# Patch layer of a four-layer network: one quarter of a direction's B products moved to ScalarE and TensorE, with the side work planned anew

## The chip, the cores and the metric

The kernel runs on one core of one Trainium2 chip. The metric is the device time of one execution in microseconds. Five engines work side by side, each through its own queue in order: TensorE (PE in the profile; PEld is its weight load), VectorE (DVE), ScalarE (ACT), GpSimd (POOL) and SyncE (SP), which here only issues DMAs.

## The reference: what is computed

The input is eight images of 96 channels and 64 x 64 pixels. Four layers follow one another, each added to its input. The change touches only the third, the patch layer. For each image it convolves, samples the image at shifted places, and cuts the result into 4 x 4 patches. Each patch is scanned in four directions with its own weights:

```python
def step(hst, inputs):
    ut, dt, bt, ct = inputs
    dA = jnp.exp(dt[..., None] * A)
    hst = hst * dA + (dt * ut)[..., None] * bt[:, :, None, :]
    y = jnp.einsum('bkdn,bkn->bkd', hst, ct)
    return (hst, y)
```

There are 192 inner channels d and 16 states n. So each step needs, for each channel and state, a decay `exp(dt*A)`, a **B product** `(dt*u)*b`, the recurrence, a **C product** `h*c`, and a sum over the states. The four directions are then added, normalised, gated and projected.

## The kernel before, in words

**Chunks and groups.** The patch layer (`layer2`, line 1190) works on 64 chunks: 8 images of 8 chunks, each of 512 pixels (32 patches of 16 steps). A chunk has 48 groups: four directions n = 0 to 3 (12 groups each; n = 0 and 1 form one pair, n = 2 and 3 the other). A group holds 32 channels by 4 states on the 128 partitions and two further sets of states side by side on the free axis, so a tile is 128 x 2 x 512. Two groups (part 0 and part 1) cover the 16 states of 32 channels. A chunk's 48 groups stand in slots B to B+47, with B = 48 times the chunk's number; below, **slot s** means slot B+s, counted modulo 48, as neighbouring chunks overlap. Direction 1 holds slots 6 to 17, direction 3 slots 30 to 41; directions 0 and 2 hold the rest.

**One slot.** `WideSlots.slot` (line 451) issues one slot's work, and each engine runs it in that order:

- SP loads `dd` (the step sizes d and the products d*u, spread over partitions) for the group six slots ahead, one load for two groups.
- ACT computes the two decays of the next group into the PSUM tile `ps_d` (line 466, two instructions of 128 x 512). `ps_d` has three buffers, so they wait for the C product of the group two slots back, which reads the same buffer.
- DVE runs the scan of this group over 1024 elements (line 1584), writing over `ps_d`, and then the C product of the previous group (line 490) into `dbu`.
- PE sums the states of the group two slots back into `ps_y` (line 373, two 512-column matmuls, four records in the trace).
- POOL makes the B product of the group two slots ahead into `dbu` (line 485, 128 x 1024; eight buffers).

`LATE2` names groups whose scan writes over `dbu` instead, whose C product is made by POOL in place, one slot after the scan, and whose sum on PE comes a slot later. It is empty before the change.

**Side work.** All else is planned by hand with `sl.at(slot, engine, function)`. Within a slot the order is: decays, "first" (ACT), scan, sum, "pe", "act", B product, C product, "pool", "dve", "sp". All side matmuls share one PSUM buffer `ps_a`, so each waits until ACT has copied out the one before it. The items that matter here:

- `front`: the offset convolution (line 1280, 18 matmuls), its copies (line 1294), Gelu (line 1312), the two offset rows (lines 1321 and 1332), Tanh (line 1341) with the scaling after it (line 1348), and bilinear sampling on POOL (lines 1359 to 1383). Gelu, Tanh and Silu (line 1469) each come with two activation table loads.
- `inner` and `both` (lines 1403 to 1432): the products u, and the rows b and c, which go to DRAM and come back spread as `brep` and `crep`.
- `pair` (line 1474): the step sizes of two directions by softplus: Abs and Relu (1495, 1496), Exp, add one, Ln, less one (1502 to 1513) on ACT, and four kinds of POOL products on three blocks (lines 1522 to 1538).
- `gates` and `end`: gate, normalisation, output, residual.

Of the kernel before, what the change touches and what calls it, by code (L numbers as in the profile page):

```python
# [13 lines left out]
ALU = mybir.AluOpType  # L14
# [232 lines left out]
AHEAD2, SPREAD2 = 6, 4  # L247
LATE2 = ()

# [192 lines left out]
class WideSlots(Slots):  # L442
# [8 lines left out]
    def slot(self, t):  # L451
        nc, G = self.S.nc, self.groups.get
        g = G(t + self.ahead)
        if g and g.part:
            g.dd = G(t + self.ahead - 1).dd
        elif g:
            g.dd = new(self.pool, [128, 2, NW], "dd", bufs=self.spread)
            nc.sync.dma_start(
                g.dd.rearrange("p x l -> p (x l)"),
                g.steps().unsqueeze(1).to_broadcast([self.gc, 128 // self.gc, 2 * NW]),  # L460
            )
        g = G(t + 1)
        if g:
            g.da = new(self.psd, [128, 2, NW], "ps_d")
            for i in range(2):
                nc.scalar.activation(  # L466
                    g.da[:, i, :], g.dd[:, 0, :], AF.Exp, scale=g.a[:, i : i + 1]
                )
        self.side(t, "first")
        g = G(t)  # L470
        if g:
            g.h = g.dbu if g.late else g.da
            g.scan(*(v.rearrange("p i l -> p (i l)") for v in (g.h, g.da, g.dbu)))
        g = G(t - 2)
        if g and not g.late:
            self.total(g)
        self.side(t, "pe")
        g = G(t - 3)
        if g and g.late:
            self.total(g)  # L480
        self.side(t, "act")
        g = G(t + 2)
        if g:
            g.dbu = new(self.pool, [128, 2, NW], "dbu", bufs=8)
            nc.gpsimd.tensor_tensor(  # L485
                g.dbu, g.dd[:, 1:2, :].to_broadcast([128, 2, NW]), g.b(), ALU.mult
            )
        g = G(t - 1)
        if g:
            (nc.gpsimd if g.late else nc.vector).tensor_tensor(g.dbu, g.h, g.c(), ALU.mult)  # L490
        for engine in ("pool", "dve", "sp", "end"):
            self.side(t, engine)
# [697 lines left out]
def layer2(S, src, dst, st_in, st_out, images, cp, W, ready, finish):  # L1190
# [3 lines left out]
    with ExitStack() as ctx:  # L1194
# [31 lines left out]
        pads, samples = [], []  # L1226
        for k in range(4):
            t = new(cp, [CH, 10, IW + 2], f"pad{k}")
# [15 lines left out]
        def front(ch, b, pad, xs, c, B):  # L1244
# [4 lines left out]
            def load():  # L1249
                ch["x"] = new(fp, [CH, 10 * IW], "xl")  # L1250
                r = 8 * c - 1
# [49 lines left out]
            for m, slots, last in (  # L1301
                (0, ((-81, 1), (-80, 2), (-79, 1), (-78, 1), (-77, 1), (-76, 1), (-75, 2)), -74),
                (1, ((-67, 1), (-66, 2), (-65, 1), (-64, 1), (-63, 1), (-62, 1), (-61, 2)), -60),
            ):
# [9 lines left out]

            sl.at(B - 60, "act", gelu)

            def offset(a):
# [15 lines left out]

                sl.at(B - 59 + a, "pe", pe)
                sl.at(B - 58 + a, "first", act)

# [12 lines left out]

            sl.at(B - 57, "act", tanh)  # L1350
            sl.at(B - 56, "act", place)

# [45 lines left out]
            def inner(j):  # L1398
# [16 lines left out]

                sl.at(B - 23 + j, "pe", pe)
                sl.at(B - 22 + j, "first", act)

# [11 lines left out]
            def both_out():  # L1430
                ch["bc"] = new(fp, [128, NW], "bc")
                nc.scalar.copy(ch["bc"], ch["pa"])
# [4 lines left out]

            sl.at(B - 20, "pe", both)
            sl.at(B - 19, "first", both_out)
            sl.at(B - 19, "sp", both_store)  # L1440

        def gates(ch, pad, T):
            x = pad[:, 1:9, 1 : IW + 1]

            def gate(m):
# [15 lines left out]

                sl.at(T + m, "pe", pe)
                sl.at(T + 1 + m, "first", act)

# [6 lines left out]

            sl.at(T + 2, "act", silu)

        def pair(ch, xs, n, T):
# [4 lines left out]
            def first(j):  # L1479
# [11 lines left out]
                def act():  # L1491
                    if j == 0:
                        st["e"] = new(fp, [128, BLK, NW], "sp_e")
                        st["m"] = new(fp, [128, BLK, NW], "sp_m")
                    nc.scalar.activation(st["e"][:, j, :], st["p"], AF.Abs)
                    nc.scalar.activation(st["m"][:, j, :], st["p"], AF.Relu)

                sl.at(T - 26 + j, "pe", pe)
                sl.at(T - 25 + j, "first", act)

# [14 lines left out]
            for m, run in enumerate((exp, one, ln, less)):  # L1515
                sl.at(T - 22 + m, "act", run)

            def block(j):
                e, m, w, s = (lambda k=k: st[k][:, j, :] for k in "emws")

                def add():
                    nc.gpsimd.tensor_tensor(m(), m(), s(), ALU.add)  # L1522

# [3 lines left out]
                def delta():  # L1527
                    if j == 0:
                        pr["d"] = new(fp, [128, BLK, 2, NW], "delta", bufs=2)
                    nc.gpsimd.tensor_tensor(pr["d"][:, j, 0, :], m(), w(), ALU.subtract)  # L1530

# [16 lines left out]
                for i, run in enumerate((add, lost, delta, delta_u)):  # L1548
                    t = BLK * i + j
                    t = T - 18 + t + (t > 4)  # L1550
                    sl.at(t, "pool", run)
                sl.at(t + 1, "act", edges)

            for j in range(BLK):
                first(j)
                block(j)
            return pr

        def direction(ch, pr, xs, k, n, T):
# [43 lines left out]
            def steps_of(h, g):  # L1603
                row = (n % 2) * DI + h * HD + g * GC2
                j, r = row // 128, row % 128
                return lambda: pr["d"][r : r + GC2, j].rearrange("p x l -> p (x l)")

            for h in range(2):
                for i in range(6):
# [5 lines left out]
                        c=lambda p=part: dr["c"][:, 2 * p : 2 * p + 2, :],  # L1615
                        y=y_of(h, e), scan=scan, late=24 * (n // 2) + 12 * h + e in LATE2,
                    )

        def end(ch, im, b, c, B):
# [64 lines left out]
            def residual():  # L1684
                ch["xo"] = new(fp, [CH, 8, IW], "xo")
                nc.sync.dma_start(
# [38 lines left out]
            for h in range(2):  # L1725
                columns(h)
                centred(h)
                sl.at(B + 76 + h, "pool", lambda h=h: gated(h))
                sl.at(B + 87 + h, "pe", lambda h=h: out(h))
            for t, engine, run in (  # L1730
                (54, "pe", variance), (55, "first", root), (56, "dve", scaled),
                (84, "sp", residual), (89, "pe", plus), (90, "first", sum_out),
                (90, "dve", stats), (91, "sp", store),
            ):
                sl.at(B + t, engine, run)
            if c == NC - 1:
                GroupStats(S, sl, B + 90, st_out[:, b, :], lambda: im["bns"], fp, psa, "ps_a")

# [4 lines left out]
        def piece(n, b, q, m, T0, T):  # L1743
            p, at = {}, slice(q * 1024, q * 1024 + 1024)

            def load():
                p["y"] = new(wp, [128, 1024], "dbu", bufs=8)
                if m < SPREAD2:
# [28 lines left out]
        for n, b in enumerate(images[ready:]):  # L1777
            GroupStats(
                S, sl, 48 * n - 6, st_in[:, b, :], lambda n=n: late_bns[n], fp, psa, "ps_a", nm[b]
            )  # L1780

        for n, b in enumerate(images):
            im = {"bns": new(fp, [CH, NC, 6], f"bns{n % 2}")}
            for c in range(NC):
                i, ch = NC * n + c, {}
                B, pad, xs = PER * i, pads[i % 4], samples[i % 2]
                front(ch, b, pad, xs, c, B)
# [5 lines left out]

                gates(ch, pad, B + (42 if b == images[-1] and c == NC - 1 else 61))
                end(ch, im, b, c, B)
# [443 lines left out]
```

## Time and profile before

| what | value |
|---|---|
| median of 20 runs | 18146.22 us (18098.46 to 18187.52) |
| the profiled execution | 18165.51 us |
| its span, first to last instruction | 18163.7 us |
| first and last scan of the patch layer (line 1584), from the span's start | 3866.8 and 14301.3 us |
| DVE busy over the span | 16214.0 us (89%) |
| POOL busy | 14801.8 us (81%) |
| PE busy | 13670.5 us (75%) |
| ACT busy | 10057.1 us (55%) |

The profiled execution stands 19 us above the median, inside the spread of the runs. The shares over the span are averages over four different layers; the patch layer is the stretch between the two scans in the table, 10434 us. A line of the groups gives: code line, engine, operation, output and inputs, shapes, count, then busy us, mean ns of one, and after the bar the engine's idle time before such instructions. A line of the timeline gives start, duration, engine and instruction, and in brackets the idle time before it. An instruction's recorded time overlaps a little with the next one's on the same engine, so the distance between starts is what one costs in a full queue.

### The profile page before, as it was taken

To read this page: it belongs to the slowest core of one execution; us is meant where nothing else is said; L and a number is where in the kernel's file an instruction comes from. 1 tells how busy PE (TensorE), PEld (TensorE's weight loads), DVE (VectorE), ACT (ScalarE), POOL (GpSimd) and SP (SyncE) were. 2 spreads that over 40 slices of the span, in tenths; PEclk is the share of its full clock that TensorE was granted. 3 is DMA by queue.
4 is the path that set the end of the run, shared out by engine and by line. 5 is a ranking of instruction groups with operands and counts; after the bars stand their busy time and mean duration, and the time that the engine had idled before them with its cause. 6 is when DMAs were issued, how large, how long until landed. Compare 5 with 4: busy or idle time off the path is not lost. (4 is left out here: it accounts for less than half of the span.)

```text
span 18163.7 us, 125849 instructions
## 1 busy us (share of the span) xinstructions
PE 13670.5 (75%) x32964; PEld 4889.5 (27%) x32964; DVE 16214.0 (89%) x11111; ACT 10057.1 (55%) x16056; POOL 14801.8 (81%) x8876
## 2 busy tenths in 40 slices
PE   8999998968888888888888888888888634433332
PEld 2223233722222222222222222222222211111111
DVE  7999998679999999999999999999999766667667
ACT  6777775556666666666666666666666311111100
POOL 7999996059999999999999999999999555565555
PEclk8999998989999999999999999999999866666666
DMA  7888886366566565666656565666656444444444
GB/s 126 149 150 149 150 150 116 64 155 138 131 136 136 132 138 131 137 132 137 135 133 135 132 139 130 137 134 134 137 131 138 111 137 144 140 142 136 136 128 121
DMA packets 802718, 2437.25 MB, mean 134 GB/s; under 512 B 259122, under 2 KB 260863, under 8 KB 734829
## 3 DMA queue, kind: packets, MB, share of 16 engines
q1 hardware_dynamic: 654541, 1976.06, 52.2%
q0 software_dynamic: 147456, 453.13, 8.3%
q8 instruction: 262, 4.29, 0.1%
q14 instruction: 459, 3.76, 0.1%
HBM read 1116.39 MB, written 104.46 MB: 67 GB/s over the span
## 5 line engine op out<-in xcount | busy, mean ns | idle before, releaser
L373 PE MATMUL ps_y<-dbu,k_red 128*96 128x512 f32 x15360 | 7588.9, 619 | 1479.1 <-DVE dbu L490 1430.5
L485 POOL TENSOR_TENSOR dbu<-dd,brep 128x1024 f32<-128x1024 f32 x3072 | 7216.8, 2361 | 223.4 <-PE ps_y L373 106.9
L1584 DVE TENSOR_TENSOR_SCAN ps_d<-ps_d,dbu 128x1024 f32<-128x1024 f32 x3072 | 7015.4, 2284 | 127.0 <-issue 106.9
L466 ACT ACTIVATE ps_d<-dd,l_alog 128x512 f32<-128x512 f32 x6144 | 4241.6, 691 | 3352.9 <-DVE dbu L490 3236.4
L373 PEld LDWEIGHTS ps_y<-dbu,k_red 128*96 128x96 f32 x15360 | 2343.4, 166 | 6386.5 <-DVE dbu L490 3384.6
L490 DVE TENSOR_TENSOR dbu<-ps_d,crep 128x1024 f32<-128x1024 f32 x3072 | 3702.2, 1205 | 0.0
L2073 POOL DMA_INDIRECT v<-t,idx x2304 | 2190.4, 951 | 1594.2 <-DVE s L2100 778.3
L355 POOL TENSOR_TENSOR dbu<-dd,brep 128x1024 f32<-128x1024 f32 x768 | 1793.3, 2353 | 134.5 <-DMA dd<-delta 114.0
L2100 DVE TENSOR_REDUCE s<-v 128x864 f32<-128x3456 f32 x256 | 1555.0, 6074 | 320.3 <-remote 217.5
L2091 DVE TENSOR_TENSOR v<-v,ps_w 128x3456 f32<-128x3456 f32 x256 | 958.3, 3743 | 831.5 <-ACT ps_w L2083 755.3
L735 DVE TENSOR_TENSOR_SCAN ps_d<-ps_d,carry,dbu 128x512 f32<-128x512 f32 x1184 | 1452.8, 1272 | 87.7 <-POOL dbu L355 69.1
L2119 ACT COPY smp<-ps_t 128x768 f32<-128x768 f32 (+1 forms) x512 | 244.4, 529 | 1769.9 <-remote 1031.6
L1280 PE MATMUL ps_a<-pad,woff 96*96 96x512 f32 x2304 | 1145.8, 598 | 26.8 <-ACT pad L1257 24.3
L337 ACT ACTIVATE ps_d<-dd,l_alog 128x512 f32<-128x512 f32 x1536 | 999.2, 681 | 151.7 <-DMA dd<-delta 100.3
L2111 PE MATMUL ps_t<-k_ident,s 128*128 128x128 f32 (+1 forms) x1792 | 321.8, 332 | 930.6 <-issue 565.2
L365 DVE TENSOR_TENSOR dbu<-ps_d,crep 128x512 f32<-128x512 f32 x1344 | 850.5, 674 | 0.0
L1522 POOL TENSOR_TENSOR sp_m<-sp_m,sp_s 128x512 f32<-128x512 f32 x384 | 487.8, 1270 | 370.9 <-ACT sp_s L1510 370.9
L1925 PE MATMUL ps_u<-k_ident,oc 27*128 27x27 f32 x256 | 33.0, 252 | 868.9 <-ACT oc L1920 844.2
L1908 PE MATMUL ps_a<-xpad,l_om 96*27 96x512 f32 x1152 | 590.8, 666 | 3.0 <-issue 2.9
L1280 PEld LDWEIGHTS ps_a<-pad,woff 96*96 96x96 f32 x2304 | 373.5, 164 | 667.8 <-issue 551.5
L2111 PEld LDWEIGHTS ps_t<-k_ident,s 128*128 128x128 f32 (+1 forms) x1792 | 249.6, 169 | 1057.7 <-issue 841.0
L2142 PE MATMUL ps_o<-smp,l_w 128*96 128x512 f32 (+1 forms) x896 | 461.7, 673 | 95.1 <-ACT smp L2119 70.3
(278 smaller groups left out, 15920.3 us busy)
## 6 DMA issues: line engine op xcount, KB each, us to landing
dd<-delta SPq DMA_DIRECT2D x2304, 512.0 KB
brep<-bcd SPq DMA_DIRECT2D x256, 1024.0 KB
crep<-bcd SPq DMA_DIRECT2D x256, 1024.0 KB
v<-t,idx POOLq DMA_INDIRECT x2304
xo<-x SPq DMA_DIRECT2D x128, 192.0 KB
x<-xo SPq DMA_DIRECT2D x128, 192.0 KB
bcd<-bc SPq DMA_DIRECT2D x64, 256.0 KB
xn<-x SPq DMA_DIRECT2D x64, 192.0 KB
```

Of the source, the lines that this page charges most:

```text
L337: nc.scalar.activation(da, g.dd[:, 0, :], AF.Exp, scale=g.a[:, i : i + 1])
L355: nc.gpsimd.tensor_tensor(g.dbu, g.dd[:, 1:2, :].to_broadcast([128, 2, NW]), g.b(), ALU.mult)
L373: self.S.nc.tensor.matmul(y, self.red[:, HD - self.gc * (g.n + 1) : 2 * HD - self.gc * (g.n + 1)], g.dbu[:, i, :], start=first and i == 0, ...
L466: nc.scalar.activation(g.da[:, i, :], g.dd[:, 0, :], AF.Exp, scale=g.a[:, i : i + 1])
L485: nc.gpsimd.tensor_tensor(g.dbu, g.dd[:, 1:2, :].to_broadcast([128, 2, NW]), g.b(), ALU.mult)
L490: (nc.gpsimd if g.late else nc.vector).tensor_tensor(g.dbu, g.h, g.c(), ALU.mult)
L735: nc.vector.tensor_tensor_scan(out, da, dbu, carry[:, n + i : n + i + 1] if c else 0.0, ALU.mult, ALU.add)
L1280: nc.tensor.matmul(ch["pk"][:HD, :], woff[:, k, m * HD : (m + 1) * HD], pad[:, dy : dy + 8, dx : dx + IW], start=k == 0, stop=k == KT - 1,)
L1584: nc.vector.tensor_tensor_scan(out[:, way], da[:, way], dbu[:, way], 0.0, ALU.mult, ALU.add)
L2073: nc.gpsimd.indirect_dma_start(out=st["v"][:, k].rearrange("p q c -> p (q c)"), out_offset=None, in_=flat, in_offset=bass.IndirectOffsetOn ...
L2091: nc.vector.tensor_tensor(v3, v3, ps_w[:, g % 2, j * 4 * KT : (j + 1) * 4 * KT] .unsqueeze(2) .to_broadcast([128, 4 * KT, CH]), ALU.mult,)
L2100: nc.vector.tensor_reduce(st["s"], st["v"].rearrange("p k q c -> p k c q"), mybir.AxisListType.X, ALU.add,)
```

## The change

**A quarter of the B products of directions 1 and 3.** In the six part-1 groups of each of these directions (slots 7, 9, ..., 17 and 31, 33, ..., 41) POOL makes only the first half of the B product (128 x 512). The other half is made with the steps on the partitions:

- `rows` (new, two times a pair): PE transposes d*u of the pair's second direction, four 128 x 128 blocks, and multiplies the sampled pixels with four b columns (two small matmuls) into `ps_a`; ACT copies both out (`turned`, `turnedb`).
- `scaled` (new, 16 times a pair): one ACT copy of 192 elements with a scale per partition, written with a stride of four elements into `prod`.
- `turn` (new, once per such group): four PE transposes of 128 x 128 bring `prod` back into the second half of the `ps_d` tile. They stand in PE's queue ahead of the sum, in the slot before the scan.
- The second decay of such a group goes into the second half of `dbu` (SBUF), and the scan is split into two of 512, the second with the two inputs in exchanged places.

**Five late groups.** `LATE2 = (14, 16, 21, 38, 40)`: five C products of 128 x 1024 a chunk go from DVE to POOL.

**Buffers.** `dbu` has seven buffers instead of eight, there are three padded chunks instead of four, `xl`, `bc` and `xo` share one buffer, and Relu writes straight into `delta` (the tile `sp_m` goes).

**Side work.** Most items get other slots:

| item | slots before | slots after |
|---|---|---|
| convolution, halves 0 and 1 | 15 to 21, 29 to 35 | 22 to 28, 32 to 37 |
| Gelu (ACT) | 36 | 38 |
| offset rows: PE; copy | 37, 38; 38, 39 | 40, 41; 41, 42 |
| Tanh; scaling after it | 39; 40 | 42; 42 |
| u: PE; b and c: PE | 25 to 27; 28 | 16 to 18; 12 |
| gate: PE; Silu | 13, 14; 15 | 2, 5; 9 |
| softplus on ACT, n = 0 / 1 | 26 to 29 / 2 to 5 | 23 to 26 / 47 to 2 |
| softplus on POOL, n = 0 / 1 | 30 to 42 / 6 to 18 | 26 to 37 / 2 to 13 |
| gating on POOL; output on PE | 28, 29; 39 to 41 | 14, 15; 29 to 31 |

```diff
-LATE2 = ()
+LATE2 = (14, 16, 21, 38, 40)
...
+                da = g.dbu if g.turn and i else g.da
+                nc.scalar.activation(da[:, i, :], g.dd[:, 0, :], AF.Exp, scale=g.a[:, i : i + 1])
+            if g.turn:
+                g.turn(g.da[:, 1, :])
...
+            if g.turn:
+                g.scan(g.h[:, 0, :], g.da[:, 0, :], g.dbu[:, 0, :])
+                g.scan(g.h[:, 1, :], g.dbu[:, 1, :], g.da[:, 1, :])
+            else:
+                g.scan(*(v.rearrange("p i l -> p (i l)") for v in (g.h, g.da, g.dbu)))
...
-            g.dbu = new(self.pool, [128, 2, NW], "dbu", bufs=8)
+            g.dbu = new(self.pool, [128, 2, NW], "dbu", bufs=7)
+            n = 1 if g.turn else 2
             nc.gpsimd.tensor_tensor(
-                g.dbu, g.dd[:, 1:2, :].to_broadcast([128, 2, NW]), g.b(), ALU.mult
+                g.dbu[:, :n, :], g.dd[:, 1:2, :].to_broadcast([128, n, NW]), g.b()[:, :n, :],
+                ALU.mult,
             )
...
-            sl.at(B - 60, "act", gelu)
+            sl.at(B - 58, "act", gelu)
...
-            sl.at(B - 57, "act", tanh)
-            sl.at(B - 56, "act", place)
+            sl.at(B - 54, "act", tanh)
+            sl.at(B - 54, "act", place)
...
+            def rows(q):
+                def pe():
+                    pr["pa"] = new(psa, [128, NW], "ps_a")
+                    for k in range(2):
+                        at = slice((2 * q + k) * 128, (2 * q + k + 1) * 128)
+                        for j in range(1, BLK):
+                            c = k * 256 + (j - 1) * 128
+                            nc.tensor.transpose(
+                                pr["pa"][:, c : c + 128], pr["d"][:, j, 1, at], S.ident
+                            )
+                        nc.tensor.matmul(
+                            pr["pa"][:, k * 256 : k * 256 + HS2], xs[:CH, n, at],
+                            bc_w[:, n, 2 * n + 1, 3:NS:4], start=True, stop=True,
+                        )
...
+                sl.at(T - 10 + q, "pe", pe)
+                sl.at(T - 9 + q, "first", act)
...
+            def scaled(m):
...
+                    nc.scalar.activation(
+                        pr["prod"][:, k, :, q], pr["du"][:, k, :], AF.Copy,
+                        scale=pr["bt"][:, k, q : q + 1],
+                    )
...
+            for t, count in (
+                (-7, 2), (-5, 3), (-4, 1), (-3, 1), (-2, 1), (-1, 1), (0, 1), (2, 1), (3, 1),
+                (4, 2), (5, 2),
+            ):
+                for _ in range(count):
+                    sl.at(T + t, "act", scaled(m))
+                    m += 1
...
+            def turn_of(h, g):
+                at = h * HD + g * GC2
+
+                def run(out):
+                    for k in range(4):
+                        nc.tensor.transpose(
+                            out[:, k * 128 : (k + 1) * 128],
+                            pr["prod"][:, k, at : at + GC2, :].rearrange("p c s -> p (c s)"),
+                            S.ident,
+                        )
```

Here T is the pair's first slot: B for directions 0 and 1, B+24 for directions 2 and 3.

## Prediction

> **What bounds the kernel now.** I read the busy times of a stretch inside the patch layer first, then the groups, then the timeline of single slots. In the stretch (columns: us, then PE, PEld, DVE, ACT, POOL busy, granted clock, DMA share, GB/s) DVE is busy 2967 of 3000 us, POOL 2828. Three groups carry it:
>
> ```profile
> 6000.00:9000.00 3000.00, 2532.81 (x5491) 842.67 (x5490) 2967.39 (x1806) 2017.09 (x2909) 2827.86 (x1535) 0.99 0.61 134
> ```
>
> ```profile
> L485 POOL TENSOR_TENSOR dbu<-dd,brep 128x1024 f32<-128x1024 f32 x3072 | 7216.8, 2361 | 223.4 <-PE ps_y L373 106.9
> L1584 DVE TENSOR_TENSOR_SCAN ps_d<-ps_d,dbu 128x1024 f32<-128x1024 f32 x3072 | 7015.4, 2284 | 127.0 <-issue 106.9
> L490 DVE TENSOR_TENSOR dbu<-ps_d,crep 128x1024 f32<-128x1024 f32 x3072 | 3702.2, 1205 | 0.0
> ```
>
> First and last scan start 10434.5 us apart: 3.398 us a slot, 163.1 us a chunk of 48. The timeline shows what a slot is made of, around Gelu and Tanh:
>
> ```profile
> 7251.51 2.29 DVE L1584 TENSOR_TENSOR_SCAN ps_d<-ps_d,dbu 128x1024 f32<-128x1024 f32 x1
> 7253.70 1.21 DVE L490 TENSOR_TENSOR dbu<-ps_d,crep 128x1024 f32<-128x1024 f32 x1
> 7254.82 2.29 DVE L1584 TENSOR_TENSOR_SCAN ps_d<-ps_d,dbu 128x1024 f32<-128x1024 f32 x1
> ...
> 7258.92 2.30 DVE L1584 TENSOR_TENSOR_SCAN ps_d<-ps_d,dbu 128x1024 f32<-128x1024 f32 x1 [0.70 <-issue]
> ```
>
> ```profile
> 7251.63 1.42 ACT L466 ACTIVATE ps_d<-dd,l_alog 128x512 f32<-128x512 f32 x2 [1.90 <-DVE dbu L490]
> 7252.98 0.76 ACT L1294 ACTIVATE off<-ps_a,sh,sc 96x512 f32<-96x512 f32 x1
> 7253.76 1.28 ACT L1312 ACT_TABLE_LOAD   x1
> 7255.05 1.06 ACT L1312 ACTIVATE off<-off 96x1024 f32<-96x1024 f32 x1
> 7256.12 1.28 ACT L1313 ACT_TABLE_LOAD   x1
> 7257.42 1.42 ACT L466 ACTIVATE ps_d<-dd,l_alog 128x512 f32<-128x512 f32 x2
> ...
> 7263.73 0.57 ACT L1332 COPY fr<-ps_a 96x512 f32<-96x512 f32 x1
> ...
> 7267.98 1.41 ACT L466 ACTIVATE ps_d<-dd,l_alog 128x512 f32<-128x512 f32 x2
> 7269.33 1.13 ACT L1348 ACTIVATE fr<-fr,half 96x1024 f32<-96x1024 f32 x1
> ```
>
> A scan costs 2.19 us (start to next start), a C product 1.12, a slot 3.31. ACT's decays start when the C product frees `ps_d`, 0.12 us after a scan starts; a scan can follow 1.50 us after its decays start (7257.42 to 7258.92). So ACT may be some 1.8 us late before DVE waits. Gelu, with two table loads, is later than that: DVE waits 0.70 us. The waits name three such stalls a chunk, 64.0 us in 6000, or 1.74 a chunk. The bound is DVE plus what ACT's table loads add to it.
>
> **The change, part by part, per chunk.**
>
> Late groups: five C products leave DVE, 5 x 1.12 = **-5.6 us**. POOL gets five, at 2.35 us each by the first layer's row for the same product (line 360, 2352 ns), 11.8 us in all.
>
> Turned groups: POOL makes twelve half products less. A half costs about 1.27 (line 1522, 128 x 512), a whole one 2.36: -13.1. POOL's busy time is 2827.86/3000 x 163.1 = 153.7 us a chunk, so it falls to about 152.4. That is still under DVE. A late product must wait for its scan, so POOL loses its lead at slots 15, 17, 22, 39 and 41; in slots 15, 17, 22 and 41 it has 4.7 us of work against 2.2 of DVE, but 2.4 against 3.3 in the slot after, and a B product has two slots until its scan. Covered; if it weren't, each such slot could cost about 1 us. The sum of a late group comes one slot later, and its `dbu` is wanted again two slots after that, so seven buffers suffice.
>
> Split scans: 12 times, two of 512 for one of 1024. The first layer's scans of 512 without carry take 1206 ns (into PSUM) and 1204 (into SBUF), so where an operand lies costs nothing there. Less the overlap of 0.09, 2 x 1.12 - 2.19 = 0.04: **+0.5**. The form with a carry takes 1268 ns, which as a bound gives +2.0; no row has the inputs exchanged. I take 0.5, the form without carry being the one used.
>
> Work on ACT: 32 scaled copies of 192 elements. The copy at line 1396 reads with a stride of 16 bytes and takes 1.10 us for 512, the scaling at line 1348 takes 1.13 for 1024 contiguous. Counting from the 32-element copy of line 1546 (0.24 us), that gives 0.53 or 0.38 for 192, less 0.1 of overlap 0.43 or 0.28. I take 0.43, as the stride is the same: 13.8 us, and 2 for the copies of `rows`. ACT was busy 109.7 of 163.1. They are spread one to three a slot; where softplus stands too (slots 47 to 2) a slot holds 1.35 of decays, 1.49 at most of softplus and 0.43: 3.27 of 3.31. Hidden, by 0.04. From 0.6 us a copy it would begin to show, about 0.5 us a chunk.
>
> The Trainium skill ("SBUF — State Buffer", "Door 1: The DMA port swizzle") says that SBUF has lines of 16 bytes and wants two hits a line, which speaks against a write with 16 bytes between elements. Here the row at line 1396 agrees for reads: about 1.8 ns an element against 0.9. Without the rule's penalty the copies would be 9 us by the row of line 1348, with it 13.8 by that of line 1396; either is hidden.
>
> Work on PE: 64 transposes and 16 small records. The trace has transposes only in the last layer:
>
> ```profile
> 17496.69 1.70 PE L2111 MATMUL ps_t<-k_ident,s 128*96 128x128 f32 x14
> 17506.87 1.70 PE L2111 MATMUL ps_t<-k_ident,s 128*96 128x128 f32 x7 [8.49 <-DVE s L2100]
> ```
>
> In a stream one costs 0.12 us, after an 8.5 us pause 0.24. I take 0.12: in the patch layer the granted clock is 0.99 and PE pauses little. The tightest place is slots 14 to 17. From scan 14: turn 0.5, skip term 0.9, sum 1.7, `rows` 1.2, sum 1.7, `rows` 1.2, turn 0.5 plus 0.3 to land: 8.0 us, with 8.9 until scan 17 (3.32 + 2.24 + 3.32). Hidden by 0.9.
>
> Table loads: here the cost lies. Stalls of today go (**-1.74**): Silu, in slot 9, stands behind the normalising product (1.2 us on DVE in slot 8), and 3.7 us of it fit. But Gelu and Tanh now stand beside late groups, in which DVE has less to do.
>
> - Gelu, slot 38. Today scan 36 to the scan after Gelu takes 7258.92 - 7251.51 = 7.41 us. In slot 37 a copy that waits for PE and two edge copies now end 0.5 after the decays could start, one edge copy (0.2) is added, and one decay goes to SBUF (about 0.1 less): 8.0. DVE needs 3.32 + 2.24 until scan 40, as the C product of group 38 is POOL's: 5.6. Stall **2.4**.
> - Tanh, slot 42, now with its scaling in the same slot. From scan 41, PE finishes the first offset row (1.0), a sum (1.7), and the second row (1.7 + 0.3); its copy starts at 4.8. From there to the decays 4.25 (7263.73 to 7267.98), the scaling 1.04, decays to scan 1.50: scan 44 at 11.6. DVE alone: 2.24 + 3.32 + 3.32 = 8.9. Stall **2.7**, or 2.1 if PE were never late (the copy after two decays, the first copy and two scaled ones, at 4.2).
>
> New stalls 5.1. Convolution, u, gates and output keep their instructions and DMAs; their new slots fall where ACT and PE have room. The shared `xl` buffer makes SP wait for a store issued 11 slots before. DMA share (0.61) hardly moves.
>
> **Sum:** -5.6 + 0.5 - 1.74 + 5.1 = -1.75 us a chunk, x 64 = -112; before the first slot, ten scaled copies add 4 at most, which I leave out. From the profiled execution, 18165.5 - 112 = 18053; it stands 19 above the median, so the prediction on the median is 18146 - 112 = **18034**.
>
> **Rivals.**
>
> 1. *Transposes cost PE too much (slower).* Place: slots 14 to 17 and 38 to 41, 16 transposes each. At 0.24 each, 16 x 0.12 = 1.9 more: the first place misses by 1.0, the second adds up to 1.9 to the Tanh chain, 2.9 in all, so +1.2 a chunk: **18220**. It turns at 0.20 a transpose (32 x 0.08 less the margin of 0.9 is 1.75). For it: they come in bursts of four behind waits. Against: the stream of fourteen, and the clock. By the Trainium skill ("TensorE: Matmul & The Clock Gate", "Part 4: PE-mode transpose") a transpose takes about 275 ns in a kernel; an estimate from that figure puts the change at a loss of some 150 us. The row of fourteen in 1.70 us contradicts it for a stream.
> 2. *Table loads stall no more than today.* If ACT gets ahead during the stalled scans more than I see, the two stalls stay at 0.7 each: -5.6 + 0.5 - 1.74 + 1.4 = -5.4, **17800**. Against: the queue in order, which today gives its 0.70.
> 3. *No gain to be measured.* The two halves of a `ps_d` or `dbu` tile wait for each other, so that the transposes follow the first decay (0.8 later, once in each tight place), or the copies cost 0.6 to 0.7: 1 to 1.6 us of the 1.75 given back, **18100 to 18140**. Against: today loads and edge copies of different blocks of `delta` don't stall one another.
>
> **How the numbers follow.** Forecast (-60 to -190 us) 0.52; rival 2 (-190 to -350) 0.13; rival 3 0.18, of which 0.02 is still faster by more than 0.2%; rival 1 0.17. A measurement of this kernel can tell about 0.2%, 36 us, from no change. Faster 0.67, same 0.16, slower 0.17. Range: from 17890, half way to rival 2, to 18220, rival 1's own price.
>
> **What would show it.** Scan to scan in a chunk: slots 15, 17, 22, 39, 41 near 2.2, Silu's stall gone, waits of 2 to 3 us before scans 40 and 44 with ACT's table loads ahead of them. If waits before scans 7 to 17 name PE's transposes, rival 1 is right. If the waits are under 1 us, rival 2. POOL idle must not shrink to nothing.

## The result, and the profile after

The changed kernel takes **18383.84 us** (median of 7 runs, 18350.1 to 18401.84), the kernel before beside it 18141.12 (47 runs): ratio 1.0131, 95% interval 1.0118 to 1.0143. It is 243 us slower; 112 us faster was forecast. The profiled execution took 18412.51 us, 247 more than the one of before. Between the first and the last scan of the patch layer lie 10653.2 us against 10434.4: 219 of the 247 are there. The first scan starts 11 us later, and some 17 are behind the last.

The same stretch as before, columns as there (us, then PE, PEld, DVE, ACT, POOL busy, granted clock, DMA share, GB/s):

```profile
6000.00:9000.00 3000.00, 2661.42 (x6798) 1048.14 (x6798) 2829.05 (x1888) 2231.22 (x3567) 2740.84 (x1588) 0.95 0.60 132
```

DVE is busy 138 us less, though the layer lasts longer, so it waits. The granted clock fell from 0.99 to 0.95. The groups of the page:

```profile
L491 POOL TENSOR_TENSOR dbu<-dd,brep 128x1024 f32<-128x1024 f32 (+1 forms) x3072 | 6408.7, 2096 | 120.6 <-ACT ps_d L467 96.4
L1638 DVE TENSOR_TENSOR_SCAN ps_d<-ps_d,dbu 128x1024 f32<-128x1024 f32 (+1 forms) x2752 | 5460.9, 1986 | 370.1 <-issue 271.3
L1596 ACT ACTIVATE prod<-turned,turnedb 128x192 f32<-128x192 f32 x2048 | 1150.7, 628 | 0.0
L497 POOL TENSOR_TENSOR dbu<-dbu,crep 128x1024 f32<-128x1024 f32 x320 | 755.3, 2360 | 342.1 <-DVE dbu L1638 342.1
L1638 DVE TENSOR_TENSOR_SCAN dbu<-ps_d,dbu 128x1024 f32<-128x1024 f32 x320 | 728.5, 2276 | 148.3 <-ACT ps_d L467 148.3
```

The idle time of DVE ahead of scans was 127 us; now it is 370 ahead of those into `ps_d` and 148 ahead of the late ones, which are counted apart. Where it lies in a chunk is read from the distances between scan starts. Below, "slot n" is the distance from scan n to scan n+1, the median over chunks 10 to 54; a full slot is 3.32.

| slot | before | forecast | after | e3 (below) |
|---|---|---|---|---|
| turned, not late (7, 9, 11, 13, 31, 35, 37) | 3.32 (37: 4.10) | 3.36 | 3.58 | 3.58 |
| behind a late group, no wait: 22; with a turned scan 15, 17, 41 | 3.32 | 2.2 | 2.20; 2.46 | 2.20; 2.46 |
| 16 (before: stall behind Silu) | 3.91 | 3.32 | 3.30 | 3.30 |
| 26 | 3.32 | 3.32 | **4.84** | 3.32 |
| 39 (Gelu) | 3.32 | 4.6 | 4.94 | 4.94 |
| 43 (Tanh) | 3.31 | 6.0 | **8.10** | 5.30 |
| mean chunk | 163.1 | 161.3 | 166.9 | 162.9 |

DVE's timeline around Gelu and Tanh, in chunk 25 (scan 39 is the pair at 8183.75, scan 44 the last line):

```profile
8183.75 1.22 DVE L1638 TENSOR_TENSOR_SCAN ps_d<-ps_d,dbu 128x512 f32<-128x512 f32 x1
8185.08 1.23 DVE L1638 TENSOR_TENSOR_SCAN ps_d<-dbu,ps_d 128x512 f32<-128x512 f32 x1
8188.69 2.29 DVE L1638 TENSOR_TENSOR_SCAN dbu<-ps_d,dbu 128x1024 f32<-128x1024 f32 x1 [2.39 <-ACT ps_d L467]
...
8200.02 1.21 DVE L497 TENSOR_TENSOR dbu<-ps_d,crep 128x1024 f32<-128x1024 f32 x1
8205.90 2.30 DVE L1638 TENSOR_TENSOR_SCAN ps_d<-ps_d,dbu 128x1024 f32<-128x1024 f32 x1 [4.67 <-issue]
```

DVE waits 2.39 us behind Gelu, as forecast, and 4.67 behind Tanh, 2 more than forecast. PE's timeline in the same place shows why:

```profile
8184.96 1.94 PE L373 MATMUL ps_y<-dbu,k_red 128*96 128x512 f32 x4
8189.11 0.50 PE L1569 MATMUL ps_a<-k_ident,delta 128*128 128x128 f32 x2 [2.22 <-ACT turnedb L1583]
...
8191.33 3.62 PE L1328 MATMUL ps_a<-off,l_off 96*96 96x512 f32 x4
8194.75 2.60 PE L373 MATMUL ps_y<-dbu,k_red 128*96 128x512 f32 x4
8197.18 1.88 PE L1328 MATMUL ps_a<-off,l_off 96*96 96x512 f32 x4
```

The same four matmuls of an offset row take 3.62 us the first time and 1.88 the second. Four stretches of that place, with the columns of the stretch above (the clock is third from the end):

```profile
8185.94:8189.36 3.42, 1.20 (x5) 0.35 (x4) 1.03 (x2) 3.38 (x6) 3.42 (x2) 1.00 1.02 183
8189.36:8192.77 3.41, 3.41 (x14) 2.46 (x13) 3.41 (x3) 2.77 (x6) 2.12 (x2) 0.50 0.71 240
8192.77:8196.18 3.41, 3.41 (x5) 1.13 (x4) 3.31 (x3) 1.19 (x3) 2.95 (x2) 0.50 0.63 123
8196.18:8200.00 3.82, 3.82 (x10) 1.47 (x9) 3.82 (x3) 2.39 (x5) 2.52 (x2) 1.00 0.24 60
```

The clock is halved for 6.83 us, two stretches of 3.41. In the 3.41 us ahead of them PE stood still for 2.22, since the second `rows` needs `ps_a`, whose copy by ACT stands behind Gelu. In the first half-rate stretch PE is busy all the time, up to 8191.33 with transposes and small matmuls alone, and the clock stays at half for another. The first offset row takes 1.7 us longer, the sum behind it 0.7, and Tanh waits for the second row, which stands behind both.

The other new stall, in slot 26, has the same root. All engines, slots 21 to 26 of the same chunk:

```profile
8127.42 1.96 PE L1287 MATMUL ps_a<-pad,woff 96*96 96x512 f32 x4
8131.02 3.46 PE L373 MATMUL ps_y<-dbu,k_red 128*96 128x512 f32 x4 [1.65 <-DVE dbu L497]
...
8139.01 0.58 ACT L1693 COPY yy<-ps_y 96x512 f32<-96x512 f32 x1 [3.27 <-PE ps_y L373]
...
8142.36 2.30 DVE L1638 TENSOR_TENSOR_SCAN ps_d<-ps_d,dbu 128x1024 f32<-128x1024 f32 x1 [1.44 <-POOL delta L1530]
```

PE waits 1.65 us for a C product, beside the late group 21; the next sum takes 3.46 us instead of 1.88, at a granted clock of 0.51 from 8131.4 to 8134.8. The copy of the patch columns (`yy`) waits 3.27 us for PE at the head of ACT's queue, the last parts of softplus stand behind it, and POOL and DVE wait for those. The trace's clock records, over 44 chunks, have a half-rate stretch of 3.41 us that begins in slot 24 in 39 of them, and one of 6.59 on average in slot 40 in 43. Before, neither place has one. The chunks themselves show what a stretch costs: slot 26 lasts 4.84 or more in the 39 chunks with one in slot 24, and 3.32 in the five without; slot 43 lasts 8.12 (median) in the 40 chunks with 6.83 us at half rate, 6.43 in the three with 3.41, and 5.23 in the one without. Half-rate stretches elsewhere, such as those that begin in slot 45 in 40 chunks, leave their slots at 3.32.

### The profile page after: what moved, and what is told of

The parts are those of the page before. It is cut to its first block, busy times and chain, and to the rows that moved or that the text cites. A ratio compares the mean times of both kernels' runs of the same rounds, so it can differ in the third digit from the quotient of the medians.

```text
span 18410.7 us, 139011 instructions
## 1 busy us (share of the span) xinstructions
PE 14313.7 (78%) x38084; PEld 5681.3 (31%) x38084; DVE 15971.3 (87%) x11559; ACT 10979.4 (60%) x18616; POOL 14728.8 (80%) x9195
## 4 chain that ended last, share of the span: by engine, by line
PE 28%; DVE 25%; ACT 20%; issue 14%; another core or an unknown queue 10%; DMA 2%; POOL 1%; DVEq 0%; SPq 0%; ACTq 0%; POOLq 0%
DVE ps_d L1638 12%; PE ps_y L373 11%; DVE dbu L497 7%; ACT ps_d L467 5%; PE ps_a L1977 2%; ACT prod L1596 2%; PE ps_a L1328 2%; PE ps_k L644 2%; DMA dd<-delta 2%; DVE ps_d L742 1%; PE ps_d L1667 1%; DVE v L2160 1%; DVE s L2169 1%; ACT sp_s L1517 1%
## 5 line engine op out<-in xcount | busy, mean ns | idle before, releaser
L491 POOL TENSOR_TENSOR dbu<-dd,brep 128x1024 f32<-128x1024 f32 (+1 forms) x3072 | 6408.7, 2096 | 120.6 <-ACT ps_d L467 96.4
L1638 DVE TENSOR_TENSOR_SCAN ps_d<-ps_d,dbu 128x1024 f32<-128x1024 f32 (+1 forms) x2752 | 5460.9, 1986 | 370.1 <-issue 271.3
L467 ACT ACTIVATE ps_d<-dd,l_alog 128x512 f32<-128x512 f32 x5376 | 3714.9, 691 | 1741.0 <-DVE dbu L497 1142.7
L355 POOL TENSOR_TENSOR dbu<-dd,brep 128x1024 f32<-128x1024 f32 x768 | 1794.1, 2355 | 142.8 <-DMA dd<-delta 109.7
L1596 ACT ACTIVATE prod<-turned,turnedb 128x192 f32<-128x192 f32 x2048 | 1150.7, 628 | 0.0
L337 ACT ACTIVATE ps_d<-dd,l_alog 128x512 f32<-128x512 f32 x1536 | 999.4, 681 | 164.7 <-DMA dd<-delta 111.7
L497 POOL TENSOR_TENSOR dbu<-dbu,crep 128x1024 f32<-128x1024 f32 x320 | 755.3, 2360 | 342.1 <-DVE dbu L1638 342.1
L1638 DVE TENSOR_TENSOR_SCAN ps_d<-dbu,ps_d 128x512 f32<-128x512 f32 x768 | 943.8, 1229 | 76.8 <-ACT ps_d L467 1.8
L1667 PE MATMUL ps_d<-k_ident,prod 128*128 128x128 f32 x3072 | 543.1, 303 | 513.9 <-ACT ps_d L467 504.9
L1638 DVE TENSOR_TENSOR_SCAN dbu<-ps_d,dbu 128x1024 f32<-128x1024 f32 x320 | 728.5, 2276 | 148.3 <-ACT ps_d L467 148.3
L1530 POOL TENSOR_TENSOR delta<-delta,sp_s 128x512 f32<-128x512 f32 x384 | 489.5, 1275 | 365.6 <-ACT sp_s L1517 365.6
```

The costliest lines, as they stand in the source:

```text
L355: nc.gpsimd.tensor_tensor(g.dbu, g.dd[:, 1:2, :].to_broadcast([128, 2, NW]), g.b(), ALU.mult)
L467: nc.scalar.activation(da[:, i, :], g.dd[:, 0, :], AF.Exp, scale=g.a[:, i : i + 1])
L491: nc.gpsimd.tensor_tensor(g.dbu[:, :n, :], g.dd[:, 1:2, :].to_broadcast([128, n, NW]), g.b()[:, :n, :], ALU.mult,)
L1596: nc.scalar.activation(pr["prod"][:, k, :, q], pr["du"][:, k, :], AF.Copy, scale=pr["bt"][:, k, q : q + 1],)
L1638: nc.vector.tensor_tensor_scan(out[:, way], da[:, way], dbu[:, way], 0.0, ALU.mult, ALU.add)
```

## The experiments

The experiments ran on several chips. On those of e5 to e8 and of e9 and e10 the kernel before takes 17306 and 17302 us, on the others 18121 to 18152. e3 and e8, the same kernel but for hidden copies, have chunks of 162.87 and 162.90 us on two of them, so chunks are compared directly, and times as ratios to the kernel before on the same chip.

**e1 and e2: what does a split scan cost?** Both are the kernel before with the changed kernel's twelve split scans alone; e2 also exchanges `da` and `dbu` in the second (the edit shown is that of e1).

```diff
+            if g.split:
+                g.scan(g.h[:, 0, :], g.da[:, 0, :], g.dbu[:, 0, :])
+                g.scan(g.h[:, 1, :], g.da[:, 1, :], g.dbu[:, 1, :])
```

> The kernel before, with one edit: in the twelve part-1 groups a chunk of directions 1 and 3 the scan of 1024 is issued as two of 512, each half with the inputs in their usual places. In the changed kernel such a split scan takes 2.46 us to the next instruction, where I had reckoned 2.24. Theory A (the exchanged inputs of the second scan, or its two producers, keep it from overlapping the first): here a split scan costs 2.24, 0.04 more than a whole one, 0.5 us a chunk and some 30 us in all, 18170. Theory B (any second scan of 512 waits for the first to drain): 2.46 here too, 3.1 us a chunk, 200 us in all, 18340.

> As the split run, but the second scan of each such group takes its two inputs in exchanged places: first the B product from SBUF, then the decay from PSUM. It computes a wrong recurrence in these halves (decay and product trade roles); its time is what counts. Both halves still come from the same engines as before the change. If the exchange is guilty: 1.32 us from the first scan to the second, 2.46 for both, 3.1 us a chunk, 18340. If it is not the exchange but the two producers (PE and ACT) that the second scan waits for in the changed kernel: 2.24 and 18170, as in the plain split if theory A holds.

e1: ratio 1.0066 (1.0043 to 1.0089), e2 1.0074 (1.0053 to 1.0094), so 119 and 134 us more. The times lie between the two theories. The exchange costs nothing, the split does: in both a turned slot lasts 3.52, and the second scan starts 1.253 us after the first. The changed kernel first, then e1:

```profile
8075.21 1.21 DVE L1638 TENSOR_TENSOR_SCAN ps_d<-ps_d,dbu 128x512 f32<-128x512 f32 x1
8076.52 1.23 DVE L1638 TENSOR_TENSOR_SCAN ps_d<-dbu,ps_d 128x512 f32<-128x512 f32 x1
8077.66 1.21 DVE L497 TENSOR_TENSOR dbu<-ps_d,crep 128x1024 f32<-128x1024 f32 x1
```

```profile
8105.25 2.48 DVE L1588 TENSOR_TENSOR_SCAN ps_d<-ps_d,dbu 128x512 f32<-128x512 f32 x2
8107.64 1.21 DVE L494 TENSOR_TENSOR dbu<-ps_d,crep 128x1024 f32<-128x1024 f32 x1
```

From the first half to the C product it is 2.45 us in the one and 2.39 in the other, where an unsplit scan takes 2.19. In the trace the second half waits on DVE's own count of finished instructions. In the changed kernel it mostly waits for ACT as well, through a semaphore instruction between the halves: the 705 pairs with one start 1.323 us apart, the 63 without, all in slot 33, 1.245. The chunk of e1 is 164.9, and the stalls of before in slots 16 and 40 shrank by 0.2, which gave some of it back.

**e7: is it the shared tile?** The kernel before, in which every group's `ps_d` is two tiles of 512 and every scan and C product is split.

```diff
-            g.da = new(self.psd, [128, 2, NW], "ps_d")
+            g.da = [new(self.psd, [128, NW], f"ps_d{i}") for i in range(2)]
...
+            for i in range(2):
+                g.scan(g.da[i], g.da[i], g.dbu[:, i, :])
```

> The kernel before with the two halves of every ps_d tile as two tiles of 512 (same banks, three buffers each), so that all scans and all C products are issued as two of 512. In the split run the second scan waited 1.25 us after the first began, with a wait for DVE's own count ahead of it; in the first layer, whose halves are two tiles, 1.13 without such a wait. Theory I (the wait comes from both halves being one tile, so that the second half waits for the first to drain): 1.12 to 1.14 here. Theory J (something else of this layer, such as the reversed order or the shapes): 1.25. The C products also come in two, so the kernel is slower either way: 0.04 for the scans and 0.06 to 0.2 for the products in each of 48 slots, 18450 to 18900.

A single run took 17515.33 us, 1.012 of before, less than was expected. The halves now follow each other as in the first layer:

```profile
8100.73 2.33 DVE L1585 TENSOR_TENSOR_SCAN ps_d<-ps_d,dbu 128x512 f32<-128x512 f32 x2
8102.97 1.26 DVE L491 TENSOR_TENSOR dbu<-ps_d,crep 128x512 f32<-128x512 f32 x2
```

A pair takes 2.24, its halves start 1.13 apart, and the wait on DVE's own count is gone in all but 56 of the 3072 pairs. So 0.12 us comes with the two halves being one `ps_d` tile, and some 0.07 more in the changed kernel with the semaphore instruction. Not every shared tile does this: the late groups of the first layer scan into the two halves of one `dbu` tile in SBUF, and there the second half does not wait for DVE and starts 1.14 us after the first (16 pairs without carry, kernel before). Why the PSUM tile does and the SBUF tile doesn't, no run shows. The kernel of e7 is slower because all 48 groups pay: a slot is 3.43.

**e3: the clock.** The changed kernel with matmuls of zero weights, which add nothing to the sums, in PE's two pauses: two behind a convolution matmul of slot 23, three in slot 39.

```diff
+                        if m == 0 and k == 1:
+                            for _ in range(2):
+                                nc.tensor.matmul(
+                                    ch["pk"][:HD, :], zero, pad[:, 0:8, 0:IW], start=False, stop=False
+                                )
...
+                    for _ in range(3):
+                        nc.tensor.matmul(ch["y", 1][:HD, :], zero, xs[:CH, 0, :], start=False, stop=False)
```

> The changed kernel plus matmuls with zero weights in the two pauses of PE that stand before its half-rate windows: two after the second convolution tap (slot 23), added into the open group in ps_a, and three after the sum in slot 39, added into ps_y. They add zeros and change nothing in the output. Theory C (the pauses halve TensorE's granted clock, and the slow matmuls behind them make the stalls): the granted clock in the patch layer goes from 0.95 to about 0.99, the wait of 1.5 us in slot 26 goes, the one before scan 44 falls from 4.8 to about 2.7 us; -3.6 us a chunk, -230 in all, 18150. Theory D (PE is short of time there, whatever its clock): ten more records cost 4.3 us of PE a chunk in the two places, the stalls stay or grow; 18384 or up to 18600.

18143.13 us, ratio 0.9995 (0.9982 to 1.0007): more work on PE makes the kernel some 240 us faster. The same stretch, and scan 44 of chunk 25:

```profile
6000.00:9000.00 3000.00, 2706.13 (x7154) 1059.70 (x7153) 2901.20 (x1939) 2292.61 (x3656) 2811.51 (x1632) 0.98 0.61 135
```

```profile
8106.72 2.30 DVE L1645 TENSOR_TENSOR_SCAN ps_d<-ps_d,dbu 128x1024 f32<-128x1024 f32 x1 [1.90 <-issue]
```

The half-rate stretches of slots 24 and 40 are gone from all 44 chunks, slot 26 is 3.32 again, without a wait, and Tanh's stall is 1.98. Gelu's stays at 2.5: PE has no part in it.

**e4: do transposes hold the clock up?** The changed kernel with its 64 transposes as ordinary matmuls with the identity.

```diff
-                        nc.tensor.transpose(
+                        nc.tensor.matmul(
...
-                            S.ident,
+                            S.ident, start=True, stop=True,
```

> The changed kernel with its 64 transposes a chunk issued as ordinary matmuls against the identity (same output, two records each instead of one, so 7 us more of PE work a chunk). In the changed kernel the second half-rate stretch (slots 40 and 41) lasts two windows of 3.4 us although PE is full in the first of them, with transposes and small matmuls. Theory E (transposes do not count as activity for the clock): the stretch shrinks to one window and the wait before scan 44 from 4.8 to about 3.5 us; the added PE work stays mostly covered; 18300 to 18380. Theory F (the clock does not distinguish them): the stretch stays at 6.8 us, and the added records cost as rival 1 reckoned, 1 to 3 us a chunk; 18450 to 18580.

18413.42 us, ratio 1.0145 (1.0124 to 1.0165), between the two ranges and no faster, though the clock rose to 0.98: the stretches at slot 40 are gone, and Tanh's slot falls from 8.10 to 5.83. But slot 16 becomes 5.03 and slot 39 5.41, and slot 26 stays at 4.85, as its pause has no transposes in it. What the longer stay on PE costs at slots 14 to 17 is the place of rival 1. PE's pause ahead of slot 40 (here in chunk 25):

```profile
8189.23 0.71 PE L1569 MATMUL ps_a<-k_ident,delta 128*128 128x128 f32 x4 [1.22 <-ACT turnedb L1584]
```

It is 1.22 us instead of 2.22, as the matmuls take longer. So e4 alone doesn't tell whether transposes don't count as work where the clock is decided, or the pause was too short. The changed kernel's own trace, over the same 44 chunks, speaks for the first. Cut into windows of 3.41 us, it has 43 at half rate that begin in slot 40: PE is busy for 0.98 or more of each, with matmuls of 512 columns for 0.45 (median), and after 40 of them the next window is at half rate too. After the 151 windows at half rate that matmuls of 512 columns fill to 0.97 or more, the next is always at full rate. The matmuls of four columns that stand between the transposes aren't told apart from them.

**e5 and e6: the late groups alone,** on the kernel before, three and five of them (two edits, in this order).

```diff
-LATE2 = ()
+LATE2 = (13, 21, 28)
...
-LATE2 = ()
+LATE2 = (14, 16, 21, 38, 40)
```

> The kernel before with one edit: LATE2 = (13, 21, 28), three late groups a chunk, none next to an activation table load; nothing is turned and no side work moved. POOL gets 3 x 2.31 = 6.9 us on its 153.7 a chunk, 160.6 in all. Theory G (the late groups carry the whole gain of the change, and POOL can take three without the turned products): DVE loses 3 x 1.12 = 3.4 us of 163.1, POOL's 160.6 becomes the limit or nearly; 160.1 to 160.8 a chunk, 150 to 190 us less, 17960 to 18000. Theory H (late products make POOL lose its lead and DVE waits for B products, or PE pauses and its clock halves): no gain or a loss, 18150 to 18300.

> The kernel before with the change's five late groups alone, LATE2 = (14, 16, 21, 38, 40). POOL's work would be 153.7 + 5 x 2.31 = 165.3 us a chunk, over today's 163.1. Theory G: POOL is the limit, 165 us a chunk, 18230 to 18290. If POOL's two spare slots are enough cover after all, DVE's 163.1 - 5.6 plus the stalls of Gelu and Tanh beside late groups (5.1 less today's 1.4) decides: 161.2, 18030.

e5: **0.990** (0.9884 to 0.9917), a chunk of 160.4; it beats both kernels. e6: 1.0061 (1.0045 to 1.0078), a chunk of 164.9. Both are where theory G put them. Their stretches, in this order:

```profile
6000.00:9000.00 3000.00, 2581.50 (x5598) 885.10 (x5597) 2956.08 (x1779) 2049.23 (x2961) 2998.81 (x1616) 0.97 0.61 137
```

```profile
6000.00:9000.00 3000.00, 2496.42 (x5427) 855.24 (x5426) 2857.96 (x1696) 1988.53 (x2882) 3000.00 (x1612) 0.98 0.61 134
```

POOL is busy 2998.81 and 3000.00 of 3000 us. Three late products just fill it; with five DVE waits for it, in slots 18 to 20 above all. So the exchange that the change makes (POOL gives half products to ACT to take C products) has a reason, but three of the five late groups could be had without it.

**e8: are the scaled copies hidden?** e3 without them; `prod` holds zeros, so a quarter of the B products of directions 1 and 3 is left out.

```diff
-                        pr["prod"] = new(fp, [128, 4, DI, HS2], "prod")
+            pr["prod"] = still
```

> The kernel of the run with zero-weight matmuls in PE's pauses, without the 32 scaled copies a chunk: prod is zeroed once and the transposes turn zeros, so that a quarter of the B products of directions 1 and 3 is left out. If ScalarE's scaled copies (0.43 us each, 13.6 a chunk) are hidden, as I reckoned: no change, 18130 to 18145. If they cost what they take in the crowded slots: up to 3 us a chunk less, 17950.

0.9995 (0.9986 to 1.0005), a chunk of 162.90, the same slots as e3. Hidden.

**e9 to e12: which late groups earn their 1.12 us?** All are e3 with another `LATE2`.

> The changed kernel with the five zero-weight matmuls of e3 in PE's two pauses, and with the late groups 38 and 40 put elsewhere: late are 14, 16, 19, 21 and 45. Theory J (a late group beside a table load saves nothing: ACT sets the time there, so the wait of DVE grows by what its late product frees): each of the two groups now saves its 1.12 us, the waits before scans 40 and 44 shrink by 1.12 each (of 2.48 and 1.98), so the chunk falls from e3's 162.87 to 160.6 us, ratio to the kernel before 0.986. Theory K (the waits are ACT's own and keep their size wherever the late groups stand): the chunk stays at 162.9, ratio 0.9995. Theory L (POOL lacks room for four late products in eight slots): waits of DVE for POOL in slots 20 to 25 and a chunk between 161.5 and 162.5.

> As e9, but the late groups 38 and 40 are left out instead of moved: late are 14, 16 and 21, so DVE makes two products more a chunk. Theory J: these two saved nothing, so the chunk stays at e3's 162.87 us within 0.3 and the ratio to the kernel before at 0.9995 within 0.002; the waits before scans 40 and 44 are 1.12 shorter each. Theory K: DVE has 2 x 1.12 more, the chunk is 165.1, ratio 1.013.

> The changed kernel with the five zero-weight matmuls of e3, and one late group moved: 38, which stands beside Gelu, gives way to 45 (late: 14, 16, 21, 40, 45). By e9 and e10 a late group 38 saves nothing (Gelu's wait shrank by 1.12 when it went), a late group 40 saves its 1.12 (Tanh's wait did not shrink), group 45 saved its 1.12, and the wait before scan 27 in e9 came from POOL, a product behind after groups 19 and 21. Theory M (so read, each group counts by its own place): the chunk falls from e3's 162.87 to 161.75, the slot before scan 40 from 4.94 to 3.8 plus the 1.12 that slot 39 gets back in DVE work, and slot 26 stays at 3.32; ratio to the kernel before 0.9925. Theory N (any further shift of POOL's work brings another wait of 1 to 2 us): 162.9 to 164, ratio 0.9995 to 1.005.

> As e11, with the other of the two groups moved: 40 gives way to 45 (late: 14, 16, 21, 38, 45). In e9, e10 and e11 the six slots from scan 38 to scan 44 last 23.98 us each time, whatever DVE has to do in them, in e3 22.63: the sum of a late group 38 goes to PE a slot later, so the offset matmuls come 1.35 sooner. Theory P (this stretch is a chain of PE and ACT, and group 40 saves nothing in it): it stays at 22.63 without the late group 40, and group 45 saves 1.12, of which 0.75 may be given back in slot 47 as in e11: 161.75 to 162.5 us a chunk, ratio 0.993 to 0.998. Theory Q (group 40 saves its 1.12 and Tanh's wait keeps its size, as I read e10 at first): the stretch lasts 23.75, the chunk 162.9 to 163.6, ratio 0.9995 to 1.003.

| run | late | ratio | chunk | slots 14 to 26 | slots 38 to 43 | slots 44 to 47 |
|---|---|---|---|---|---|---|
| e3 | 14, 16, 21, 38, 40 | 0.9995 (0.9982 to 1.0007) | 162.87 | 40.2 | 22.63 | 13.29 |
| e10 | 14, 16, 21 | 1.0047 (1.0031 to 1.0064) | 164.25 | 40.2 | 23.98 | 13.29 |
| e11 | 14, 16, 21, 40, 45 | 1.0044 (1.0030 to 1.0058) | 163.84 | 40.2 | 23.98 | 12.91 |
| e12 | 14, 16, 21, 38, 45 | 1.0032 (1.0016 to 1.0047) | 163.83 | 40.2 | 23.44 | 13.41 |
| e9 | 14, 16, 19, 21, 45 | 1.0046 (1.0029 to 1.0063) | 164.12 | 41.1 | 23.98 | 12.14 |

Of all these readings only N, the loss, met its range. J and K both fall: the groups 38 and 40 together save 1.35 of their 2.24. M falls, N holds: each move was paid back elsewhere. P and Q both fall: in e12 the stretch from scan 38 to scan 44 lies between theirs, nearer to Q's, and the chunk above both. What the slots do say: with 38 not late the stretch from scan 38 to scan 44 lasts 23.98 us whether 40 is late (e11) or not (e10), so alone 40 saves nothing there. The traces show the order on PE: the sum of a late group 38 stands behind the first offset row, and so both rows start 1.3 to 1.4 us sooner in e3 than in e10 and e11. In e12 the rows are as early as in e3, but Tanh's copy starts only after the two decays of the slot. A late group 45 saved 1.12 in slot 46 in all three runs that had it, and e11 and e12 gave 0.75 and 1.25 back in slot 47. PE's timeline of e12 there, after Tanh's stall:

```profile
8120.03 1.96 PE L373 MATMUL ps_y<-dbu,k_red 128*96 128x512 f32 x4
8125.04 2.07 PE L1497 MATMUL ps_a<-xs,wd 97*128 97x512 f32 x2 [3.06 <-ACT delta L1510]
8126.91 3.62 PE L373 MATMUL ps_y<-dbu,k_red 128*96 128x512 f32 x4
```

During the stall PE has caught up with all its sums; then it waits 3.06 us for ACT, and the next matmuls run at half the clock. The clock records have a stretch of 6.83 us from slot 44 in all 44 chunks of e12 and in 40 of e11: a third pause, which the five matmuls do not cover. In the four chunks of e11 without it slot 47 lasts 3.30 instead of 4.07. Such a stretch costs nothing there without a late group 45: e10 has one of 6.83 us in 18 chunks, and slot 47 stays at 3.32. In e9 the stall of slot 26 is back (5.30) without any half-rate stretch near it. In chunk 25 PE works there for 14.1 us on end at the full clock before the `yy` copy, so the sums that the copy waits for are late on PE; what part the late products 19 and 21 of POOL have in that, no run shows. None of the four beats e3, and none comes near e5.

## Why the prediction was wrong

**Right.** The late groups took 1.12 from slots 15, 17, 22 and 41. POOL had room for them with the half products gone. The late product took 2.36 us, the half B product 1.28, a scaled copy 0.425 from start to start (0.43 forecast), and the copies are hidden (e8). A transpose at the full clock cost 0.11 in the stream. Silu's stall went, and Gelu's came at 2.48 where 2.4 was forecast. There is luck in that: from scan 38 to scan 40 it took 8.25 us, 0.25 more than the chain was given, and the split scan ahead of the stall takes up 0.2 of it. The thing to look for, waits before scans 40 and 44 behind table loads, was there.

**Wrong, in three terms of the sum.**

1. *Split scans, +0.5 a chunk.* Measured 0.26 each in the changed kernel, 3.1 a chunk, so 2.6 more: 166 us over 64 chunks. The row that the term was taken from, the first layer's scans of 512 into `ps_d`, is one of scans into separate tiles; the one beside it, into `dbu`, is of halves of one SBUF tile, which don't wait for each other. Those of the change are halves of one PSUM tile, and the second waits for the first to finish (e1, e2, e7). The bound of +2.0, from the form with carry, was nearer by chance and too low as well. Rival 3 had the idea that halves of a tile wait for each other, but for the transposes, not on DVE, where it costs the engine that bounds.

2. *"In the patch layer the granted clock is 0.99 and PE pauses little."* That held before. The change made the pauses itself: the late group 21, whose sum comes a slot later, leaves PE a slot without a sum, and Gelu's own forecast stall keeps `ps_a` occupied. The sum had both in it as time of DVE, and nobody asked what PE does meanwhile. It costs 1.5 in slot 26, which was not in the sum, and 2.8 in Tanh's slot (8.10 against 5.30 in e3), 2.1 of it over the forecast: 3.6 a chunk more than forecast, 230 us. e3 takes 4.0 a chunk away, some 240 us by the ratios.

3. *Tanh, 2.7.* Measured 4.78, and 1.98 where the clock holds. The term said 2.1 "if PE were never late", and that is what e3 shows. What failed is the clock at which the offset rows ran, not the queue on ACT.

Together, with Tanh's 2.1 counted once, they make 2.6 + 1.5 + 2.1 = 6.2 us a chunk, some 395 us in 64; between forecast (-112) and result (+243) lie 355. The remaining -40 has several sources that no run separates: chunks without a half-rate stretch (the mean chunk is 0.3 below that of the medians), stalls of before of 2.1 a chunk in these distances where 1.74 was counted, and on the other side the 28 us outside the scans.

**The rivals.** Rival 1 had the sign, a slow clock, and one of its two places in part. In slots 14 to 17 the transposes are hidden in the changed kernel: no wait grew there. In Tanh's chain they are slow, but the first offset row starts only 0.4 us later after scan 38 than in e3 (10.84 against 10.41); the rest of the 2.8 lies behind it, in the offset rows and the sum at half the clock. Its price of 18220 was too low, and the range with it, since it took the slow clock as a property of transposes in bursts. Rival 2 is excluded by Gelu's 2.48.

The Trainium skill ("TensorE: Matmul & The Clock Gate", "Part 1: The HAM clock gate") says that the clock is decided in windows of about 3.4 us that run free of the kernel, and that it drops to half after an idle one. The records agree: in the patch layer of the changed kernel every half-rate stretch is 3.41 us or a multiple, and all begin on one grid of that step, to within 0.02 us. They also go further than the page: a window with a pause of 1.65 us in it was enough. The same page's "Part 4: PE-mode transpose" says that transposes do not count as busy time for it in the same way; the full stretches at half rate in slot 40 agree. The prediction drew a time from that section and left this sentence of it unused.

## What to carry to other kernels

Take the price of an operation from a row with the same dependence, in the same memory, as well as the same shape: a second instruction on the other half of a PSUM tile may have to wait for the first on its own engine. Where a change makes the engine that bounds wait, ask what TensorE does in that wait: if it pauses, its clock may halve for the next microseconds, and what it then does late can become the next wait. A gain in one slot counts only once the next wait on the same chain has been worked out again; here three late groups without any side work beat the whole change.

## What was not expected of the hardware

- A pause of PE of 1.65 or 2.22 us, not a whole window, is followed by one or two windows of 3.41 us at half the clock in 39 and 43 of 44 chunks, and an offset row takes 3.62 us instead of 1.88. What share of a window must be busy was not tried.
- A window at half rate that PE filled, for about half of it with transposes and matmuls of four columns, was followed by another in 40 of 43 chunks; one filled with matmuls of 512 columns, in none of 151.
- Two scans of 512 on halves of one PSUM tile start 1.25 us apart (1.32 in the changed kernel), on two tiles 1.13, and on halves of one SBUF tile in the first layer 1.14.
- A copy of 192 elements with a scale per partition, written at a stride of 16 bytes, is recorded with 0.63 us and costs 0.425 in a queue.
